# A two-layer network on one Trainium2 core: a new hand order for layer 1's scan, the image added to the rows during dispatch, and the last normalization batch in three stages

## Chip, cores and metric

The kernel runs on one core of one Trainium2 chip. A core has five engines that run their own instruction queues in order: PE (matrix products), DVE (vectors), ACT (activations and copies), POOL (vectors, and DMAs with computed addresses) and SP (DMA issue). They synchronise by semaphores. The metric is device time in microseconds (us), the median of repeated executions. One further execution was profiled; durations come from it.

## The reference, cut to what matters

The input is x, 32 images of 128 channels and 56 x 56 pixels, in float32. T = 32 x 3136 = 100352 tokens.

```python
# layer 0: convolution, normalization, mixture of experts
x = depthwise_conv7x7(input) + dw_bias                 # then channels last
x = (x - mean) / sqrt(var + 1e-6) * ln_gamma + ln_beta # per token, over channels
topv, topi = top_k(x @ Wg + bg, 2)                     # 8 experts, 2 per token
wts = softmax(topv)                                    # wts[:, 0] also ranks the tokens
# each expert takes its first int(1.25 * T / 8) tokens in rank order
y[e] = gelu(rows[e] @ W1[e] + b1[e]) @ W2[e] + b2[e]   # 128 -> 512 -> 128
out = input + x + layer_scale * sum_over_kept(gate * y)

# layer 1: two branches on x = out of layer 0
xh = cv1_w @ x + cv1_b
l = silu(batchnorm(depthwise_conv3x3(xh)))
t = layernorm(xh tokens)                               # 3136 tokens per image
xm, z = split(t @ in_proj_w.T)                         # 256 channels each
xm = silu(causal_conv4(xm) + conv1d_b)
dt, B, C = split(xm @ x_proj_w.T);  dt = softplus(dt @ dt_proj_w.T + dt_proj_b)
for each token: h = exp(dt * A) * h + dt * B * xm;  y = (h * C).sum(16 states)
g = ((y + xm * D) * silu(z)) @ out_proj_w.T
return x + cv2_w @ concat(l, g) + cv2_b
```

## The kernel before, in words

The kernel runs five stages one after the other.

*Convolution (start to about 1535 us).* The images are turned to pixels-by-channels in eight batches of four (`fill`), convolved on PE, and each batch is normalized while the next is convolved. `norm` handles 28 / 4 = 7 columns of 112 tokens at a time (a column is two image rows): DVE takes statistics (`bn_stats`, `bn_aggr`), ACT the square root, DVE its reciprocal `rs` and the shift `nm`, ACT writes the seven normalized columns into `xa`, POOL multiplies by `lng` and adds `lnb`, SP stores `xa` to the tensor `res_d` in memory, PE transposes `xa` and multiplies by the gate's weights, and DVE adds the bias to the logits. The tokens of a column come out of the convolution with each image row reversed. The last batch has no convolution beside it: its 16 norms run alone. The order of instructions outside layer 1 is made by the language's scheduler from the order of the program.

*Routing (to about 1775 us).* Top-2, gates and slots of all tokens on DVE and ACT, while SP fills the experts' buffer `buf_d` with zeros.

*Dispatch (1775 to 3940 us).* 56 steps (`QB` = 7 values of q, eight `p0` of 14 columns). SP loads a block of rows from `res_d` into `xg0`, ACT copies it to `xg1`, DVE writes each row's gate and its place for the way back (`bi`, made by an iota on POOL), and POOL issues 28 indirect DMAs (L859) that write 128 rows each to their slots in `buf_d`. There are six pairs of `xg` buffers. The weights of layer 1 are prepared in the middle (`weights`).

*Experts (3940 to about 5880 us).* For each 512 rows of `buf_d`: transposes, two products with a GELU between them, bias and gate, and POOL's indirect DMAs (L911) add the results to the tokens' rows in `res_d`.

*Layer 1 (about 5880 us to the end).* 224 groups g of 448 tokens (7 per image). For each group there are 16 units, one for each state i of the scan. A unit is: ACT's `exp_act` (two halves of 128 channels) into one of two PSUM buffers `da`, by turns; POOL's `db_pool`, one instruction for two units, `db` = `du` x B; DVE's `scan_dve`, the recurrence along the tokens; `cmul`, the product of the states with C (`cb`); `carry_act`, which copies the last state to the next group's start; and `sum_pe`, which adds the product to the group's sum in PSUM. `MODE` gives each unit a letter: D scans in place and multiplies on DVE; P scans into an SBUF buffer `hs` and multiplies on POOL; Q is P with the scan in two halves; M scans in two halves, with the product of the first half on DVE and of the second on POOL.

All other work of a group (`PLAN`: loading, the 1x1 convolution, normalization, projections, softplus, output) and of a unit (`UNITS`) has a place: a number in units of a sixteenth of a period, relative to the group's or the unit's start. The steps of all groups are sorted by place and issued in that order under a manual schedule, so the places set the order of every engine's queue, and nothing else: an engine does its next instruction as soon as what it needs is there.

```python
todo.append((DS * g + key, len(todo), names[name], (g, *args)))            # PLAN
todo.append((DS * g + i + key, len(todo), names[name], (DS * g + i, *args)))  # UNITS
todo.sort()
```

`fetch` loads the image block `x1` and the rows `yg` (from `res_d`); `moe_pe` adds them in PSUM, undoing the reversed rows with the permutation `perm`; `moe_act` copies the sum to `x1`. `du_pool` needs `dt`, which `sp_act` writes. `rstd_dve` (L1090, L1092, L1095), `te_dve` and `yz_dve` are the other DVE work.

Of the kernel before, what the change touches and what calls it, by code (L numbers as in the profile page):

```python
# [5 lines left out]
F32 = mybir.dt.float32  # L6
I32 = mybir.dt.int32
AF = mybir.ActivationFunctionType
# [34 lines left out]
MODE = 'DQDDQDPPDDDDPDDP'  # L43
PRODS = 6
PLAN = (
    (-41.157, "fetch"),
    (-34.382, "moe_pe"),
    (-32.986, "moe_act"),
    (-28.346, "cv1_pe", "p_cvc", "cv1c"),
    (-27.384, "sq_act"),  # L50
    (-26.393, "cv1_pe", "p_cv1", "cv1t"),
    (-25.274, "cv1_act"),
    (-23.306, "var_pe"),
    (-23.291, "rstd_act"),
    (-23.185, "edges_act"),
    (-20.935, "rstd_dve", 0),
    (-20.876, "rstd_dve", 1),
    (-19.458, "rstd_dve", 2),
    (-19.126, "bc_pe"),
    (-18.367, "te_dve"),  # L60
    (-18.165, "te_act"),
    (-17.77, "z_pe", 0),
    (-16.927, "z_copy", 0),
    (-15.982, "z_pe", 1),
    (-15.86, "xm_pe", 0),
    (-15.811, "xm_pe", 1),
    (-14.784, "z_copy", 1),
    (-14.441, "z_silu"),
    (-14.388, "xm_act", 0),
    (-14.349, "xm_act", 1),  # L70
    (-13.504, "tables"),
    (-13.487, "px_pe"),
    (-11.507, "px_act"),
    (-11.215, "dt_pe", 0),
    (-10.684, "dt_pe", 1),
    (-10.326, "sp_abs", 0),
    (-9.043, "sp_abs", 1),
    (-8.458, "sp_exp"),
    (-7.656, "sp_one"),
    (-6.228, "sp_w"),  # L80
    (-5.252, "sp_pe", ("w", "e", "m")),
    (-5.135, "sp_ln"),
    (-5.019, "sp_pe", ("u",)),
    (-4.678, "lt_pe", range(0, 9)),
    (-4.117, "sp_act", 0),
    (-3.918, "sp_act", 1),
    (-3.032, "lt_act", 0),
    (-3.001, "du_pool"),
    (-2.343, "lt_act", 1),
    (2.033, "lt_silu"),  # L90
    (3.656, "dd_pe"),
    (18.599, "yz_dve", 0),
    (18.857, "yz_dve", 1),
    (23.328, "out_pe"),
    (25.003, "out_act"),
# [3 lines left out]
        (-5.892, "bc_load", "bb"),  # L99
        (-3.501, "bc_load", "cb"),  # L100
        (-2.818, "db_pool"),
        (-0.991, "exp_act"),
        (-0.076, "scan_dve"),
        (0.16, "cmul", 0),
        (1.245, "carry_act"),
        (3.662, "sum_pe"),
    ),
    (
        (-2.505, "db_pool"),
        (-0.83, "exp_act"),  # L110
        (-0.619, "scan_dve"),
        (1.229, "cmul", 0),
        (3.088, "carry_act"),
        (9.441, "sum_pe"),
    ),
    (
        (-11.504, "bc_load", "bb"),
        (-2.533, "bc_load", "cb"),
        (-2.288, "db_pool"),
        (-0.633, "exp_act"),  # L120
        (-0.074, "scan_dve"),
        (0.16, "cmul", 0),
        (1.407, "carry_act"),
        (3.828, "sum_pe"),
    ),
    (
        (-3.007, "db_pool"),
        (-1.559, "exp_act"),
        (-0.609, "scan_dve"),
        (-0.338, "carry_act"),  # L130
        (0.16, "cmul", 0),
        (2.009, "sum_pe"),
    ),
    (
        (-4.093, "bc_load", "bb"),
        (-3.639, "db_pool"),
        (-0.666, "bc_load", "cb"),
        (-0.482, "exp_act"),
        (0.865, "scan_dve"),
        (1.06, "cmul", 0),  # L140
        (1.786, "sum_pe"),
        (2.033, "carry_act"),
    ),
    (
        (-4.025, "db_pool"),
        (-1.052, "exp_act"),
        (-0.068, "scan_dve"),
        (0.16, "cmul", 0),
        (1.263, "carry_act"),
        (3.791, "sum_pe"),  # L150
    ),
    (
        (-5.791, "bc_load", "bb"),
        (-4.743, "db_pool"),
        (-2.416, "bc_load", "cb"),
        (-0.463, "exp_act"),
        (0.538, "scan_dve"),
        (0.678, "cmul", 0),
        (1.758, "carry_act"),
        (4.239, "sum_pe"),  # L160
    ),
    (
        (-5.64, "db_pool"),
        (-0.299, "exp_act"),
        (-0.211, "scan_dve"),
        (1.06, "cmul", 0),
        (5.047, "sum_pe"),
        (5.187, "carry_act"),
    ),
    (  # L170
        (-7.178, "bc_load", "bb"),
        (-4.153, "db_pool"),
        (-3.514, "bc_load", "cb"),
        (-1.218, "exp_act"),
        (-0.956, "scan_dve"),
        (0.16, "cmul", 0),
        (0.466, "carry_act"),
        (0.815, "sum_pe"),
    ),
    (  # L180
        (-4.714, "db_pool"),
        (-1.825, "exp_act"),
        (-0.406, "scan_dve"),
        (0.16, "cmul", 0),
        (0.742, "carry_act"),
        (1.653, "sum_pe"),
    ),
    (
        (-8.23, "bc_load", "bb"),
        (-5.573, "bc_load", "cb"),  # L190
        (-4.053, "db_pool"),
        (-1.1, "exp_act"),
        (-0.6, "scan_dve"),
        (0.16, "cmul", 0),
        (0.996, "carry_act"),
        (1.077, "sum_pe"),
    ),
    (
        (-3.777, "db_pool"),
        (-0.685, "exp_act"),  # L200
        (-0.409, "scan_dve"),
        (0.16, "cmul", 0),
        (1.104, "sum_pe"),
        (1.278, "carry_act"),
    ),
    (
        (-7.87, "bc_load", "bb"),
        (-4.884, "bc_load", "cb"),
        (-4.31, "db_pool"),
        (-0.985, "exp_act"),  # L210
        (-0.749, "scan_dve"),
        (1.06, "cmul", 0),
        (5.159, "sum_pe"),
        (5.275, "carry_act"),
    ),
    (
        (-4.947, "db_pool"),
        (-0.443, "exp_act"),
        (0.085, "scan_dve"),
        (0.16, "cmul", 0),  # L220
        (0.197, "sum_pe"),
        (0.205, "carry_act"),
    ),
    (
        (-19.062, "bc_load", "bb"),
        (-4.926, "db_pool"),
        (-2.209, "bc_load", "cb"),
        (-1.206, "exp_act"),
        (-0.658, "scan_dve"),
        (0.16, "cmul", 0),  # L230
        (0.202, "sum_pe"),
        (0.903, "carry_act"),
    ),
    (
        (-3.892, "db_pool"),
        (-0.158, "exp_act"),
        (0.91, "scan_dve"),
        (1.06, "cmul", 0),
        (2.205, "carry_act"),
        (2.818, "sum_pe"),  # L240
# [4 lines left out]
def tile_kernel(tc: tile.TileContext, a: dict, out: bass.AP):  # L245
# [14 lines left out]
    with (  # L260
# [6 lines left out]
        res_d = dram.tile([T, C], F32, name="res_d")  # L267

        ident = const.tile([128, 128], F32, name="ident")
        make_identity(nc, ident)  # L270
        mean_w = const.tile([128, 128], F32, name="mean_w")
        nc.vector.memset(mean_w, 1.0 / C)

        perm = const.tile([TT, TT], F32, name="perm")
        nc.vector.memset(perm, 0.0)
        for k in (HW - 1, 3 * HW - 1):
            nc.gpsimd.affine_select(
                out=perm, in_=perm, compare_op=ALU.not_equal, fill=1.0, base=-k, pattern=[[1, TT]],
                channel_multiplier=1,
            )  # L280
# [23 lines left out]
        with (  # L304
# [48 lines left out]
            def conv(b, c0):  # L353
# [21 lines left out]
                for c in range(4):  # L375
# [9 lines left out]
                    dwb[:, c0 : c0 + 4].unsqueeze(2).unsqueeze(3).to_broadcast([TT, 4, NB0, NP]), ALU.add,  # L385
                )

            def norm(b, i, q):

                w = NP // 4  # L390
                o = i * (NP + 1) + q * w
# [63 lines left out]
            for b in range(NB + 1):  # L455
                work = []
                for i in range(NB0):
                    if b > 0:
                        work += [(norm, b - 1, i, q) for q in range(4)]
                    if b + 1 < NB:  # L460
                        work.append((fill, b + 1, i))
# [1004 lines left out]
```

## Time and profile before

| | |
|---|---|
| median of 12 runs | 15852.14 us (15846.65 to 15859.02) |
| the profiled execution | 15854.85 us, its span 15853.1 us |
| busy of the span | PE 81%, DVE 70%, ACT 66%, POOL 84% |
| mean granted TensorE clock | 0.913 |
| data moved by DMA | 2520.85 MB, 159 GB/s |
| costliest group | `db`<-`du`,`bb` on POOL, 1792 instructions, 6578.1 us, 3682 ns each |
| scan in place on DVE (L1373) | 2240 instructions, 4522.6 us, 2019 ns each |
| exp on ACT (L1354) | 7168 instructions, 4540.1 us, 637 ns each |
| product with C on DVE / POOL (L1397) | 2240, 1089 ns each / 1344, 1937 ns each |
| scatters of dispatch (L859) | 1568 instructions, 1645.6 us |
| scatter-adds of the experts (L911) | 984 instructions, 1584.1 us |

The busy shares are averages over stages with different limits; each stage has to be read by itself. A row of the timeline gives an instruction's start, its duration, engine, line, operation, output <- inputs with partitions x elements, and in square brackets the engine's idle time before it with what ended that. "PE" rows of 448 columns come in pairs, since a float32 product is two instructions.

### The profile page before, as it was taken

The numbers are of one execution on the slowest core, as the hardware profiler recorded it, in microseconds if no ns is written. First come the engines' busy times: TensorE is split into PE (matmuls) and PEld (weight loads), VectorE is DVE, ScalarE is ACT, GpSimd is POOL, SyncE is SP. The second block draws the span as 40 slices with busy tenths as digits, with TensorE's granted clock in tenths as the row PEclk, the third lists the DMA queues.
The fourth block names the chain that finished last, engine by engine and source line by source line (L and its number), as shares of the span: only waits on it lengthen the run. The fifth ranks groups of instructions, "written<-read, shape, count | busy, mean of one in ns | idle before, by whom it ended". The sixth has DMA issues, their size and how long they took to land. (4 is left out here: it accounts for less than half of the span.)

```text
span 15853.1 us, 247520 instructions
## 1 busy us (share of the span) xinstructions
PE 12823.8 (81%) x92981; PEld 7167.9 (45%) x92981; DVE 11117.4 (70%) x11366; ACT 10495.1 (66%) x21038; POOL 13323.4 (84%) x6330
## 2 busy tenths in 40 slices
PE   7996200000999999999999999999999999999998
PEld 7996100000777764444444444444444444444444
DVE  2655400000111119999999999999999999999999
ACT  4554300000444448888888888888888888888888
POOL 2443477777788879999999999999999999999999
PEclk9997555555999999999999999999999999999999
DMA  8785422222555545555555556555555555555555
GB/s 267 228 237 174 172 71 71 71 71 64 68 72 70 71 64 183 185 185 185 185 184 184 184 185 185 183 184 185 182 184 185 184 185 184 185 183 184 184 183 171
DMA packets 1325280, 2520.85 MB, mean 159 GB/s; under 512 B 139352, under 2 KB 777136, under 8 KB 1316400
## 3 DMA queue, kind: packets, MB, share of 16 engines
q1 hardware_dynamic: 1127600, 2310.57, 46.9%
q0 software_dynamic: 196480, 194.45, 7.2%
q8 instruction: 732, 11.99, 0.3%
q14 instruction: 468, 3.83, 0.1%
HBM read 2129.06 MB, written 375.43 MB: 158 GB/s over the span
## 5 line engine op out<-in xcount | busy, mean ns | idle before, releaser
L1336 POOL TENSOR_TENSOR db<-du,bb 128x1792 f32<-128x1792 f32 x1792 | 6578.1, 3682 | 0.6 <-DMA bb<-bc_d 0.5
L1354 ACT ACTIVATE da<-dt,aneg 128x449 f32<-128x449 f32 x7168 | 4540.1, 637 | 376.2 <-DVE r L1095 113.0
L1373 DVE TENSOR_TENSOR_SCAN da<-da,db 128x898 f32<-128x898 f32 x2240 | 4522.6, 2019 | 0.6 <-issue 0.5
L1286 PE MATMUL py<-prod,ident 64*64 64x448 f32 x28672 | 3223.9, 547 | 126.7 <-DVE prod L1397 118.7
L1397 POOL TENSOR_TENSOR prod<-hs,cb 128x896 f32<-128x896 f32 x1344 | 2603.5, 1937 | 243.5 <-issue 154.3
L1397 DVE TENSOR_TENSOR prod<-da,cb 128x896 f32<-128x896 f32 x2240 | 2439.8, 1089 | 136.3 <-DMA cb<-bc_d 20.7
L859 POOL DMA_INDIRECT buf_d<-xg,slot x1568 | 1645.6, 1049 | 523.8 <-issue 519.3
L911 POOL DMA_INDIRECT res_d<-ys,xb x984 | 1584.1, 1610 | 359.2 <-issue 278.9
L951 PE MATMUL ept<-ident,xb 128*128 128x128 f32 (+1 forms) x984 | 189.0, 274 | 2078.6 <-DMA xb<-buf_d 2078.3
L1373 DVE TENSOR_TENSOR_SCAN hs<-da,db 128x898 f32<-128x898 f32 x896 | 1785.5, 2013 | 0.1
L1286 PEld LDWEIGHTS py<-prod,ident 64*64 64x64 f32 x28672 | 1007.5, 132 | 1564.5 <-issue 1054.2
L1126 PE MATMUL p_xm<-te,wk 128*128 128x448 f32 x3584 | 1395.6, 540 | 0.0
L903 DVE TENSOR_TENSOR ys<-py,b2t 128x512 f32<-128x512 f32 (+2 forms) x256 | 170.9, 670 | 1735.9 <-PE py L897 1498.3
L856 DVE COPY xg<-gate 128x14 f32<-128x14 f32 x112 | 20.5, 186 | 1884.5 <-DMA buf_d<-xg,slot 1848.3
L854 ACT COPY xg<-xg 128x1792 f32<-128x1792 f32 x56 | 94.5, 1688 | 1821.7 <-DMA buf_d<-xg,slot 1772.8
L951 PEld LDWEIGHTS ept<-ident,xb 128*128 128x128 f32 (+1 forms) x984 | 124.6, 143 | 2082.4 <-issue 2081.6
L897 PEld LDWEIGHTS py<-w2t,hh 128*128 128x128 f32 x7872 | 939.1, 192 | 191.6 <-issue 118.4
L897 PE MATMUL py<-w2t,hh 128*128 128x128 f32 x7872 | 988.7, 279 | 14.9 <-ACT hh L893 9.5
L1126 PEld LDWEIGHTS p_xm<-te,wk 128*128 128x128 f32 x3584 | 671.8, 189 | 665.8 <-issue 568.0
L379 PE MATMUL pc<-xc,toep 112*112 112x112 f32 (+1 forms) x8192 | 937.4, 270 | 37.4 <-ACT toep L368 33.8
L1377 DVE TENSOR_TENSOR_SCAN hs<-da,db 128x449 f32<-128x449 f32 x896 | 925.5, 1075 | 0.5 <-ACT da L1354 0.3
L1258 PE MATMUL p_l<-xh,dwd 64*64 64x224 f32 x16128 | 907.0, 352 | 22.1 <-ACT dt L1240 2.2
(241 smaller groups left out, 20282.0 us busy)
## 6 DMA issues: line engine op xcount, KB each, us to landing
bb<-bc_d SPq DMA_DIRECT2D x1792, 448.0 KB
cb<-bc_d SPq DMA_DIRECT2D x1792, 448.0 KB
toep<-toep_d SPq DMA_DIRECT2D x448, 392.0 KB
buf_d<-zero SPq DMA_DIRECT2D x28, 2275.0 KB
xb<-buf_d SPq DMA_DIRECT2D x240, 260.0 KB
xt<-in_x SPq DMA_DIRECT2D x32, 1568.0 KB
res_d<-xa SPq DMA_DIRECT2D x128, 392.0 KB
xg<-res_d SPq DMA_DIRECT2D x56, 896.0 KB
```

The source lines that it names most:

```text
L379: nc.tensor.matmul(pc[:, c, :, lo:hi], lhsT=tp[c // 2][:, c % 2, 6 - 2 * o : 8 - 2 * o, :], rhs=s4[:, c, :, lo + o - 1 : hi + o - 1], star ...
L859: apart(nc.gpsimd.indirect_dma_start(out=buf_d[:, :], out_offset=bass.IndirectOffsetOnAxis(ap=slots[k][:, o + j : o + j + 1], axis=0), in_ ...
L897: nc.tensor.matmul(py[:n, j, :], lhsT=hh[:, k, j * 128 : j * 128 + n], rhs=w2t[:, k, :], start=k == 0, stop=k == KF - 1,)
L911: apart(nc.gpsimd.indirect_dma_start(out=res_d[:, :], out_offset=bass.IndirectOffsetOnAxis(ap=xb[:n, j, C + 1 : C + 2].bitcast(I32), axis= ...
L1126: nc.tensor.matmul(p[:, :CH1], lhsT=s["wk"][:, k, hs], rhs=d["te"][:, k : k + CH1], start=k == 0, stop=k == DC - 1 and not first,)
L1258: nc.tensor.matmul(d["p_l"][r][k * HD : (k + 1) * HD, : CH1 // 2], lhsT=s["dwd"][rs, t, rs], rhs=d["xh"][rs, dy + k * R : dy + (k + 1) * R ...
L1286: nc.tensor.matmul(ps[r][h * HD : (h + 1) * HD, :CH1], lhsT=lhsT(rs, h), rhs=rhs[rs, h, :], start=start, stop=stop,)
L1336: nc.gpsimd.tensor_tensor(dbp[i // 2].rearrange("p k (h t) -> p k h t", h=2)[:, :, :, 1:], st[g]["du"].unsqueeze(1).to_broadcast(both), un ...
L1354: e = nc.scalar.activation(da[:, h * W1 : (h + 1) * W1], st[g]["dt"][:, h, :], AF.Exp, scale=s["aneg"][:, h, i : i + 1])
L1373: scans.append(nc.vector.tensor_tensor_scan(hs, da, dbs[i], 0.0, ALU.mult, ALU.add))
L1377: scans.append(nc.vector.tensor_tensor_scan(hs2[h][:, hh], da[:, hh], dbs[i][:, hh], 0.0, ALU.mult, ALU.add))
L1397: eng.tensor_tensor(w["prod"], w["hs"][0][:, :, 1:], w["cb"], ALU.mult)
```

## The change

1. Layer 1's `MODE`, `PLAN` and `UNITS` get new values. `exp_act` and `scan_dve` take a half as an argument, so that each half has its own place; `hs` has three buffers instead of two, `x1` four instead of five. The dependencies that are declared absent between halves and between carries, scans and `db` are kept in one table (`free`, `decay`). The unit that closes the group's sum is the one whose `sum_pe` comes last.
2. In dispatch, after each step's scatters, `skip` is called once or twice: half an image (14 columns) and its rows are loaded, PE undoes the reversal of the rows with `perm` and adds the transposed image, ACT copies the result and issues its store to a new tensor `sum_d`. The experts add to `sum_d`, with places (`bi`) that count each row of 56 backwards. The copy of `xg0` to `xg1` goes from ACT to DVE. Layer 1's `fetch` loads from `sum_d` alone, and `moe_pe` is four transposes.
3. `norm` becomes a generator with two pauses. For the last batch, the 16 norms are advanced in a pipeline of three stages: statistics, normalized columns, logits. There, two of the seven columns are written by DVE instead of ACT.

```diff
-MODE = 'DQDDQDPPDDDDPDDP'
+MODE = 'PPDDMDPPDDPDPDDD'
 PLAN = (
-    (-41.157, "fetch"),
-    (-34.382, "moe_pe"),
+    (-60.5589, "fetch"),
+    (-32.6293, "moe_pe"),
...
-    (-4.117, "sp_act", 0),
-    (-3.001, "du_pool"),
+    (-3.7463, "sp_act", 0),
+    (-1.8387, "du_pool"),
...
 UNITS = (
     (
-        (-5.892, "bc_load", "bb"),
-        (-3.501, "bc_load", "cb"),
-        (-2.818, "db_pool"),
-        (-0.991, "exp_act"),
-        (-0.076, "scan_dve"),
-        (0.16, "cmul", 0),
-        (1.245, "carry_act"),
-        (3.662, "sum_pe"),
+        (-3.5445, "bc_load", "bb"),
+        (-0.1591, "exp_act", 1),
+        (0.0298, "db_pool"),
+        (0.2221, "exp_act", 0),
+        (1.0278, "scan_dve", 0),
+        (3.4411, "bc_load", "cb"),
+        (3.8013, "cmul", 0),
+        (4.9139, "sum_pe"),
+        (5.2017, "carry_act"),
     ),
...
             def norm(b, i, q):
+                for part in normal(b, i, q):
+                    pass
+
+            def normal(b, i, q):
...
                 nc.vector.scalar_tensor_tensor(nm, mv[:, :, 0], -1.0, rs, ALU.mult, ALU.mult)
+                yield
...
                 for j in range(w):
+                    if b == NB - 1 and j in (2, 5):
+                        nc.vector.tensor_scalar(
+                            xa[:, j, :], xv[:, :, j], rs[:, j : j + 1], nm[:, j : j + 1], ALU.mult, ALU.add
+                        )
+                        continue
                     nc.scalar.activation(
...
                     out=res_d[col * TT : (col + w) * TT, :].rearrange("(k p) c -> p k c", p=TT), in_=xa
                 )
+                yield
...
+                if b == NB:
+                    line = [normal(*w[1:]) for w in work]
+                    for k in range(len(line) + 2):
+                        for part in reversed(line[max(k - 2, 0) : k + 1]):
+                            next(part, None)
+                    work = []
...
-                nc.gpsimd.iota(bi, pattern=[[TT, QB], [1, TT]], base=0, channel_multiplier=PT)
+                nc.gpsimd.iota(
+                    bi.rearrange("p q (r w) -> p q r w", w=HW), pattern=[[TT, QB], [HW, 2], [-1, HW]], base=HW - 1,
+                    channel_multiplier=PT,
+                )
...
+            def skip(n, h):
+                t0 = (n * TPI + h * HT) * TT
+                xt = sk.tile([C, HT * TT], F32, name="xs")
+                nc.sync.dma_start(out=xt, in_=x_d[n, :, h * HT * TT : (h + 1) * HT * TT])
+                xr = sk.tile([TT, HT, C], F32, name="xr")
+                rows = [v[t0 : t0 + HT * TT, :].rearrange("(k p) c -> p k c", p=TT) for v in (res_d, sum_d)]
+                nc.sync.dma_start(out=xr, in_=rows[0])
+                for j0 in range(0, HT, 4):
+                    w = min(4, HT - j0)
+                    p = psk.tile([TT, 4, C], F32, name="p_sk")
+                    nc.tensor.matmul(p[:, :w], lhsT=perm, rhs=xr[:, j0 : j0 + w], start=True, stop=False)
+                    for j in range(w):
+                        nc.tensor.matmul(
+                            p[:, j, :], lhsT=xt[:, (j0 + j) * TT : (j0 + j + 1) * TT], rhs=ident,
+                            start=False, stop=j == w - 1,
+                        )
+                    nc.scalar.copy(xr[:, j0 : j0 + w], p[:, :w])
+                nc.scalar.dma_start(out=rows[1], in_=xr)
...
-                    nc.scalar.copy(xgs[1][:, :, :C], xgs[0][:, :, :C])
+                    nc.vector.tensor_copy(xgs[1][:, :, :C], xgs[0][:, :, :C])
...
+                    for _ in range(-(-len(parts) // (TT // XT * (QB - q) - p0 // XT))):
+                        skip(*parts.pop(0))
...
-                        out=res_d[:, :],
+                        out=sum_d[:, :],
...
-            d["x1"] = three.tile([C, CH1], F32, name="x1", bufs=5)
-            nc.sync.dma_start(out=d["x1"], in_=x_d[n, :, q * CH1 : (q + 1) * CH1])
...
-                out=d["yg"], in_=res_d[t0 : t0 + CH1, :].rearrange("(j p) c -> p j c", p=TT)
+                out=d["yg"], in_=sum_d[t0 : t0 + CH1, :].rearrange("(j p) c -> p j c", p=TT)
...
-            nc.tensor.matmul(p[:, :CH1], lhsT=ident, rhs=d["x1"], start=True, stop=False)
             for j in range(TPC1):
-                nc.tensor.matmul(
-                    p[:, j * TT : (j + 1) * TT], lhsT=yg[:, j, :], rhs=perm, start=False, stop=j == TPC1 - 1
-                )
+                nc.tensor.transpose(p[:, j * TT : (j + 1) * TT], yg[:, j, :], ident[:TT, :TT])
...
-            hs = three.tile([128, 2 * W1], F32, name="hs", bufs=2) if MODE[i] in "PQM" else da
+                hs = three.tile([128, 2 * W1], F32, name="hs", bufs=3)
```

Not shown: all other places, the bookkeeping of `free` and `decay`, `te_tile` (which lets `te_act` be issued before `te_dve`), and `mean_w`, which shrinks to one column.

## The prediction

> **What bounds the kernel now.** I read the busy slices first, then windows cut at the stages, then the timeline of each engine, engine by engine, inside one period of layer 1, inside the last normalization and inside dispatch. The slices show which engine fills each stretch (one digit is 396 us):
>
> ```profile
> DVE  2655400000111119999999999999999999999999
> POOL 2443477777788879999999999999999999999999
> ```
>
> Cut at the stages, the windows view (busy us and instructions of each engine, granted clock, DMA share, GB/s) reads:
>
> ```profile
> core 0: us, PE busy (x) PEld busy (x) DVE busy (x) ACT busy (x) POOL busy (x), PEclk, DMA share, GB/s
> 1400.00:1535.00 135.00, 69.63 (x336) 62.60 (x336) 65.11 (x267) 78.50 (x160) 67.08 (x33) 0.50 0.19 48
> 1775.00:3940.00 2165.00, 6.10 (x16) 2.87 (x16) 38.02 (x247) 95.55 (x63) 1644.54 (x1567) 0.50 0.24 72
> 3940.00:5880.00 1940.00, 1904.99 (x10842) 1375.58 (x10842) 347.65 (x529) 820.51 (x1241) 1581.88 (x983) 0.99 0.54 70
> 8000.00:12000.00 4000.00, 3829.76 (x28279) 1797.47 (x28274) 3941.05 (x3078) 3474.07 (x7204) 3839.77 (x1383) 1.00 0.58 184
> ```
>
> In the last batch's normalization no engine is over 60% busy: a chain of latencies. Dispatch is POOL alone, PE and ACT nearly empty. The experts are PE (98%) and the change leaves their instructions alone. Layer 1 takes 9970 of the 15853 us, with DVE at 98.5%, POOL and PE at 96%, ACT at 87%. A gain there must shorten DVE and leave POOL, 4% below it, room.
>
> One period of layer 1, DVE's timeline (start, duration, ...):
>
> ```profile
> 9009.88 2.03 DVE L1373 TENSOR_TENSOR_SCAN da<-da,db 128x898 f32<-128x898 f32 x1
> 9012.01 1.09 DVE L1397 TENSOR_TENSOR prod<-da,cb 128x896 f32<-128x896 f32 x1
> 9018.08 0.14 DVE L1090 SCALAR_TENSOR_TENSOR da<-da,r 112x4 f32<-112x4 f32 x1
> ...
> 9047.06 3.94 DVE L1373 TENSOR_TENSOR_SCAN hs<-da,db 128x898 f32<-128x898 f32 x2
> 9050.91 2.01 DVE L1373 TENSOR_TENSOR_SCAN da<-da,db 128x898 f32<-128x898 f32 x1
> ...
> 9062.22 0.14 DVE L1090 SCALAR_TENSOR_TENSOR da<-da,r 112x4 f32<-112x4 f32 x1
> ```
>
> L1090 runs once per group, so the period is 9062.22 - 9018.08 = 44.14 us, and DVE has no marked idle in it: DVE is the bound. Starts overlap ends, so I count from start to start. A scan followed by independent work costs 1.93 (3.85 for two, 9047.06 to 9050.91); followed by its own product it costs 2.04 to 2.13; a product 1.0; two half scans 1.98; two yz 1.17; te 0.52. POOL in the same period:
>
> ```profile
> 9003.58 3.68 POOL L1336 TENSOR_TENSOR db<-du,bb 128x1792 f32<-128x1792 f32 x1
> 9007.21 1.94 POOL L1397 TENSOR_TENSOR prod<-hs,cb 128x896 f32<-128x896 f32 x1
> 9062.87 1.94 POOL L1245 TENSOR_TENSOR du<-dt,xm 128x896 f32<-128x896 f32 x1 [0.81 <-ACT dt L1240]
> ```
>
> Start to start: db 3.64, product 1.89, du 1.92. Eight, six and one make 42.4 us, so POOL idles about 1.7 per period, partly for ACT's dt.
>
> **Part 1, layer 1's places and modes.** Six P, one M and nine D replace four P, two Q and ten D. *DVE:* nine and a half products for ten: -0.49. One pair of half scans for two: -0.05. Scans followed at once by their own product fall from seven to three (new order u5, u8, u15; the rest have a scan, yz, te or rstd between): 4 x 0.15 = -0.60. Together 44.14 - 1.14 = 43.0. *POOL:* adds M's half product. From the rows, (3682 - 1937)/896 = 1.95 ns an element and 0.19 fixed, so 448 elements take 1.07, 1.02 start to start: 42.4 + 1.0 = 43.4. POOL thus becomes the longest queue. *PE:* the product of x with the identity goes (two instructions, 1.0 us a group), and four transposes replace four matmuls with `perm`: in the trace a matmul is two instructions, the transposes at L349 one, so 1.05 us becomes 0.5. PE falls from 42.3 to 40.7. *SP:* one load of 224 KB less per group. *ACT:* one more tiny copy (M's carry), 38.4 as before.
>
> The floor is therefore 43.4. What can lift it are the crossings between queues; I walked the new order with start-to-start costs. POOL's order is db 0, 4, 2, 10, 6, products 0, 1, 4, db 8, products 6, 7, db 12, 14, product 10, du, product 12. The loop db 2, scans u2 to u12 on DVE (29.7), product 12 (1.9), next db 0, 4, 2 (10.9) makes 42.5 and three handovers: under the floor by 0.6. The queues that share ACT: du waits for the copies of dt, which stand behind the exps of u12, and those wait for scan u10. By the walk dt is ready 0.35 us before POOL gets to du. On ACT the stretch between scan u1's end and scan u7 holds the exps of u3 to u7, both table loads, silu, abs and small copies: 14.8 us start to start, against 14.6 of DVE. That is even, with slack elsewhere. I take 43.6, 0.2 above the floor: (44.14 - 43.6) x 224 = **-121**. Ends: the floor itself, -166; ACT late, see the rivals.
>
> The three `hs` buffers for two and five to four `x1` cost no time: POOL's product 0 ends before scan u6 asks for its buffer (by 4 us of the walk), and x1 is written only at `moe_act`. `fetch` stands 19 places earlier on SP; its buffer is free by then (`moe_pe` of two groups before, 4 places earlier), so nothing queues behind a wait.
>
> **Part 2, the last batch's normalization.** Timeline of the end of that stage:
>
> ```profile
> 1518.32 2.05 DVE L403 SCALAR_TENSOR_TENSOR nm<-mv,rs 112x7 f32<-112x7 f32 x1
> 1520.45 2.81 ACT L406 ACTIVATE xa<-xc,nm,rs 112x128 f32<-112x128 f32 x5 [4.22 <-POOL xa L410]
> 1525.19 2.07 POOL L409 TENSOR_TENSOR xa<-xa,lng 112x896 f32<-112x896 f32 x1 [4.84 <-ACT xa L406]
> ```
>
> The DVE instruction for nm, 0.15 us elsewhere, takes 2.05 while POOL's product runs, and ends with it; ACT waits for it, POOL for ACT. POOL's two products and that wait make 9.0 us per norm; from the first sqrt (1400.66) to the last logits (1534.2) 16 norms take 133.5. In the pipeline nm is made a step earlier, so a step is the longest engine: POOL 4.15; ACT five xa (0.56 each), sqrt and copies, 4.0; DVE statistics 2.9, nm, logits and two tensor_scalars (0.21 each, as at L750), 3.9. POOL waits for the two tensor_scalars, so 4.9; with two steps of fill 18 x 4.9 = 88: **-45**. Ends: POOL alone, 18 x 4.3, -56; nm and both tensor_scalars each held for most of a POOL product, 18 x 7, -7. Everything after this stage (top-2, routing, zero fill) moves with it.
>
> **Part 3, the image added in dispatch.** 64 skips, two in each of the first 8 steps and one in the other 48. On PE one is 3.5 x 0.89 (a 512-wide matmul, from L890) + 14 x 0.25 (L897) = 6.6 us, 13 at the granted clock of 0.50 that this stage shows: under 850 us in 2165 where PE does nothing. ACT gives up a copy of 1.69 per step and gets four copies of about 0.6 per skip and the issue of the store. DVE takes the copy: about 1.3 us (tensor_scalar on 784 elements is 0.56), behind which the gate and place copies queue, six steps ahead of their use. SP queues two loads of 0.8 MB behind each xg load; an xg load of 0.9 MB fills the DMA engines for 3 to 4 us, so a buffer's round is load 7, PE 13, store 5, or 13 us per skip with two buffers, so two skips (26) fit in a step of 28 scatters (35.5). The last step's skip is loaded six steps ahead like its xg, so its store is done before the experts add to `sum_d`. `perm` moves in front of the first scatter: two POOL instructions of 0.3.
>
> Does 154 MB more traffic slow the scatters? The windows of POOL's scatters alone (busy, instructions, clock, DMA share, GB/s):
>
> ```profile
> 1775.00:2035.00 260.00, 197.80 (x205) 0.50 0.33 95
> 2100.00:3660.00 1560.00, 1181.50 (x1114) 0.50 0.24 71
> 3725.00:3935.00 210.00, 162.85 (x152) 0.50 0.15 48
> ```
>
> The pace is 1.27 us, then 1.40, and 1.38 in the last window, where the xg loads are over: less traffic, same pace, and the fastest stretch had most traffic. I take no cost for the traffic and **+5** for the late first scatter and `perm`. Ends: 0, and 56 x 1.3 = +73 if POOL stood still for every DVE copy. The row against that:
>
> ```profile
> 1828.40 1.46 DVE L750 TENSOR_SCALAR dwd<-ident,dw 128x128 f32<-128x128 f32 x7
> 1828.40 0.97 POOL L859 DMA_INDIRECT buf_d<-xg,slot  x1 [0.30 <-issue]
> ```
>
> Seven copies-with-scale on DVE, and the scatter takes its usual 0.97. The Trainium skill, "DMA: Bandwidth & Descriptors", section "SWDGE vs HWDGE vs iDMA", speaks against the move: VectorE in a two-port mode locks GpSimd out of the memory in which it writes descriptors. By it the sum would end nearer to the +73; by the row it stays at +5.
>
> **Sum.** The profiled execution took 15854.85 us (span 15853.1 and 1.75 around it), 2.7 above the median. 15854.85 - 121 - 45 + 5 = 15693.9; I say 15694 and leave the 2.7 in the range.
>
> **Rivals.** *The gain of layer 1 is eaten by handovers:* POOL at 99.5% leaves no room, each late dt or cb load (33.6 and 20.7 us of waits for cb in the whole run) now counts, and the period stays between 43.8 and 44.15. Then 15740 to 15815. For it: two queues within 1% of each other. Against: before, DVE ran a whole period without a gap.
>
> *ACT becomes the bound, and the kernel is slower:* place, ACT between the exps of u3 and u7. If its instructions cost their listed durations and not the start-to-start distances, the stretch is 16.0 and the period 44.4; each us over 14.6 costs 224. It decides from 15.9 (period about 44.3, which eats the -40 of the other parts); at 16.5 the time is 15855 + 179 - 40 = 15994. Against: before, ACT ran 33 us on end in the same way and held DVE up nowhere.
>
> *Transfers hold the scatters up:* 192 more of them, 3.5 us each; if POOL stood still in all, +672, about 16370. It decides from 0.84 us per transfer. Against: the pace without loads.
>
> *The pipeline isn't one:* the order outside layer 1 is made at build time, and the old order may come back: 15739, inside the range.
>
> **How the numbers follow.** Forecast (period 43.4 to 43.8, norm gain 7 to 56, dispatch 0 to 73) 0.67; handovers 0.19; ACT 0.10; transfers 0.04. 0.2% (32 us) is about what a measurement can tell from none: faster means under 15820. From the forecast and nearly all of the handover case 0.85; same 0.04; slower 0.11. The range reaches from floor and best pipeline (15635) to the end of the handover case (15815).
>
> **What would show it.** In the changed profile: L1090 every 43.6 us; POOL over 98.5% and DVE near 98.5% in layer 1, ACT's exps waiting for DVE and not DVE's scans for ACT; p_moe transposes of one instruction; POOL's two products every 4.9 us in the last norms; scatters at 1.40 with 140 GB/s around them. I am wrong if DVE's scans show waits for ACT's da or POOL's db of over 0.5 us a period, or if dispatch is longer than 2240.

## The result: 0.93% slower

The kernel after takes 15999.59 us (median of 7 runs, 15985.08 to 16016.95) against 15852.33 us for before (28 runs): a ratio of 1.0093, 95% interval 1.0084 to 1.0102. The forecast was 15694 us, faster. The profiled execution of after has a span of 15993.7 us, 140.6 more than before.

Cut by the first and last scatter and the first and last scatter-add, the two traces differ so (us; the predicted change beside it):

| stretch | before | after | change | predicted |
|---|---|---|---|---|
| start to the first scatter | 1773.6 | 1742.3 | -31 | -45 |
| first to last scatter (dispatch) | 2164.5 | 2372.1 | **+208** | +5 |
| last scatter to last scatter-add (experts) | 1943.0 | 1942.2 | -1 | 0 |
| last scatter-add to the end (layer 1) | 9971.9 | 9937.1 | -35 | -121 |

All three estimates were too good, but dispatch alone turned the sign. The slices of after (one digit is 400 us):

```profile
DVE  2657300000111117999999999999999999999999
POOL 2443455657788888999999999999999999999999
```

From the sixth to the ninth digit (2000 to 3600 us) POOL has fallen from 7 to 5 or 6: this is dispatch, which consists of POOL's work, and POOL now stands still in it. The windows view of after, with the columns of before's (busy us, instructions, clock, DMA share, GB/s):

```profile
1742.00:4115.00 2373.00, 584.29 (x2320) 396.47 (x2320) 90.51 (x319) 137.22 (x264) 1538.25 (x1568) 0.59 0.45 131
8000.00:12000.00 4000.00, 3799.21 (x27758) 1741.06 (x27761) 3903.28 (x2994) 3469.89 (x7310) 3937.21 (x1478) 1.00 0.57 179
```

POOL's own work in dispatch became shorter (1538 us for 1645) while the stage became longer. In layer 1 POOL went from 96.0% to 98.4% and VectorE from 98.5% to 97.6%: the busiest engine moved, the period hardly did.

**Where dispatch waits.** The waits view of after between 1760 and 4114 us (engine, line, what it waited for: us in total, times, longest):

```profile
POOL buf_d L916 <- DMA xg<-res_d: 352.8, 16, 43.0
```

```profile
ACT xr L900 <- remote: 1154.2, 83, 29.0
```

POOL waits for its rows, ACT for something that the profile calls remote. One such wait, on the timelines of SP, PE, ACT and POOL in turn (start, duration, ...; the bracket is the idle time before it):

```profile
2626.81 0.32 SPq L890 DMA_DIRECT2D xr<-res_d  x1
2677.86 0.33 SPq L887 DMA_DIRECT2D xs<-in_x  x1
2678.49 0.37 SPq L910 DMA_DIRECT2D xg<-res_d  x1
```

```profile
2624.42 1.02 PE L894 MATMUL p_sk<-xr,perm 112*112 112x512 f32 x2
2625.29 1.04 PE L896 MATMUL p_sk<-ident,xs 128*112 128x128 f32 x8
```

```profile
2630.93 0.59 ACT L900 COPY xr<-p_sk 112x512 f32<-112x512 f32 x1 [13.70 <-remote]
2651.22 0.59 ACT L900 COPY xr<-p_sk 112x512 f32<-112x512 f32 x1 [19.70 <-remote]
2675.72 0.59 ACT L900 COPY xr<-p_sk 112x512 f32<-112x512 f32 x1 [23.91 <-remote]
```

```profile
2689.28 1.27 POOL L916 DMA_INDIRECT buf_d<-xg,slot  x1 [18.58 <-DMA xg<-res_d]
```

In these rows L887 loads the image block (`xs`), L890 the skip's rows (`xr`) and L910 the rows to scatter (`xg`); the copies at L900 each wait for one chunk of TensorE's work (`p_sk`). Read it backwards. POOL lacks its xg at 2670.7 because SP issued that load only at 2678.49; SP stood for 51 us in front of it at a load of x, whose buffer TensorE had not finished reading. TensorE's rows say that the third chunk (2624.42 to 2626.3) was done at 2626.3; the copy that waits for nothing but that chunk starts at 2675.72. The ends of matmuls are modelled in these rows, and here they are wrong by 49 us: the trace has the semaphore that TensorE raises behind this chunk at 2675.70, so TensorE was not done. Where several skips queue, the copies follow one another every 28.0 us for a chunk of 10 matmul instructions (1861.56, 1889.56, 1917.57) and every 16.8 us for one of 6. That is 2.8 us for one matmul instruction, so a skip of 36 takes 101 us, not the 13 of the prediction. When POOL stops, TensorE catches up: in 16 of the 17 stops the waiting copies follow one another every 0.5 to 3 us from 6 to 8 us after the last scatter on (in the first, from 24 us on). Of the 256 copies, 191 fall into the 361 us of stops or the 20 us after each.

This is not new in after. In before TensorE does a little work during dispatch, the weights of layer 1; ACT and PE:

```profile
1869.34 0.37 ACT L821 COPY wo<-p_wo 128x256 f32<-128x256 f32 x1 [4.96 <-remote]
```

```profile
1864.01 1.23 PE L817 MATMUL p_wo<-cvgt,wop 128*128 128x128 f32 x4
```

Four instructions of 1.23 us in all, and the copy came 5.3 us after their start, 1.3 us an instruction, 90 us after the first scatter. The prediction took its price of a matmul from the experts' rows and halved the clock; the row of the right stage lay a few lines away. It shows half of the price paid later, but well over the 0.28 us that the experts' 128 x 128 products show (L897).

### The profile page after: what moved, and what is told of

It is laid out like the page before. It is cut to its first block, busy times and chain, and to the rows that moved or that the text cites. A ratio compares the mean times of both kernels' runs of the same rounds, so it can differ in the third digit from the quotient of the medians.

```text
span 15993.7 us, 248874 instructions
## 1 busy us (share of the span) xinstructions
PE 13307.1 (83%) x93941; PEld 7418.9 (46%) x93941; DVE 11067.9 (69%) x11231; ACT 10477.4 (66%) x21398; POOL 13431.3 (84%) x6554
## 5 line engine op out<-in xcount | busy, mean ns | idle before, releaser
L1433 DVE TENSOR_TENSOR_SCAN da<-da,db 128x898 f32<-128x898 f32 (+1 forms) x2240 | 4273.4, 1926 | 54.3 <-ACT da L1417 52.0
L1433 DVE TENSOR_TENSOR_SCAN hs<-da,db 128x898 f32<-128x898 f32 (+1 forms) x1568 | 2914.3, 1882 | 112.5 <-ACT da L1417 88.7
L916 POOL DMA_INDIRECT buf_d<-xg,slot x1568 | 1538.8, 981 | 837.0 <-issue 468.4
L1446 DVE TENSOR_TENSOR prod<-da,cb 128x896 f32<-128x896 f32 x2016 | 2185.8, 1084 | 43.7 <-DMA cb<-bc_d 6.0
L970 POOL DMA_INDIRECT sum_d<-ys,xb x984 | 1590.2, 1616 | 352.3 <-issue 279.2
L894 PE MATMUL p_sk<-xr,perm 112*112 112x512 f32 (+1 forms) x512 | 342.2, 759 | 1266.5 <-issue 758.7
L900 ACT COPY xr<-p_sk 112x512 f32<-112x512 f32 (+1 forms) x256 | 134.6, 533 | 1749.3 <-remote 1155.7
L1012 ACT COPY xc<-ept 128x512 f32<-128x512 f32 (+1 forms) x248 | 144.1, 581 | 1382.5 <-PE ept L1010 664.3
L383 PEld LDWEIGHTS pc<-xc,toep 112*112 112x112 f32 x8192 | 884.5, 185 | 45.4 <-ACT toep L372 39.1
L949 PE MATMUL ph<-xc,w1t 128*128 128x512 f32 (+1 forms) x1984 | 886.5, 589 | 0.0
```

What stands on the lines that cost most here:

```text
L383: nc.tensor.matmul(pc[:, c, :, lo:hi], lhsT=tp[c // 2][:, c % 2, 6 - 2 * o : 8 - 2 * o, :], rhs=s4[:, c, :, lo + o - 1 : hi + o - 1], star ...
L894: nc.tensor.matmul(p[:, :w], lhsT=perm, rhs=xr[:, j0 : j0 + w], start=True, stop=False)
L916: apart(nc.gpsimd.indirect_dma_start(out=buf_d[:, :], out_offset=bass.IndirectOffsetOnAxis(ap=slots[k][:, o + j : o + j + 1], axis=0), in_ ...
L949: nc.tensor.matmul(ph[:, :rows], lhsT=w1t[:, k * 128 : (k + 1) * 128], rhs=xc[:, :rows], start=True, stop=True)
L970: apart(nc.gpsimd.indirect_dma_start(out=sum_d[:, :], out_offset=bass.IndirectOffsetOnAxis(ap=xb[:n, j, C + 1 : C + 2].bitcast(I32), axis= ...
L1433: scan = nc.vector.tensor_tensor_scan(w["hs"][h][:, hh], da[:, hh], dbs[i][:, hh], 0.0, ALU.mult, ALU.add)
```

## The experiments

Theory: beside the scatters TensorE passes one matmul instruction per 2.8 us, skips don't fit in their steps, their loads hold SP's queue, and xg comes late. Rivals: the 154 MB more traffic; the longer SP queue by itself; VectorE's copy of xg.

**1. Fewer TensorE instructions, same transfers.**

```diff
-                    nc.tensor.matmul(p[:, :w], lhsT=perm, rhs=xr[...], start=True, stop=False)
-                    for j in range(w):
-                        nc.tensor.matmul(p[:, j, :], lhsT=xt[...], rhs=ident, start=False, stop=j == w - 1)
+                    nc.tensor.matmul(p[:, :w], lhsT=perm, rhs=xr[...], start=True, stop=True)
```

> The kernel after with the 14 products of x with the identity left out of every skip, so the image isn't added; every DMA of the skip (two loads, one store), ACT's copies and the product with perm stay. TensorE has 8 matmul instructions per skip left of 36 to 38. Theory 1, TensorE is slow while scatters run: in the trace of after, copies that wait for TensorE follow one another every 28.0 us for a chunk of 10 matmul instructions and every 16.8 us for one of 6, that is 2.8 us an instruction, and at once when POOL stands still. Then a skip takes 22 us instead of about 105, fits in a step of 28 scatters, POOL's waits for xg fall from 353 us to under 60, the scatters last 1990 to 2170 us instead of 2372 and the kernel takes 15620 to 15800 us. Theory 2, the traffic or SP's queue: nothing of either is taken away, so POOL waits for xg as before, scatters 2370 us, the kernel 15990 to 16005 us.

Measured: 15781.54 us, 218 less than after; scatters 2166.7 us long; no wait of POOL for xg is left, and the copies come every 5.6 us in the mean for 2 instructions, again 2.8 each:

```profile
2574.42 0.59 ACT L895 COPY xr<-p_sk 112x512 f32<-112x512 f32 x1 [5.93 <-remote]
2579.32 0.58 ACT L895 COPY xr<-p_sk 112x512 f32<-112x512 f32 x1 [4.32 <-remote]
2585.62 0.58 ACT L895 COPY xr<-p_sk 112x512 f32<-112x512 f32 x1 [5.71 <-remote]
```

Traffic and SP's queue, all of it still there at 143 GB/s, and VectorE's copy cost the scatters nothing. All three rivals fall.

**2. TensorE work beside scatters, without the skips.**

```diff
+            def extra(k):
+                p = psk.tile([128, 4 * C], F32, name="p_sk")
+                cols = [C, 4 * C, C][k // 19]
+                for j in range(5 if k < 38 else 10):
+                    if k < 38:
+                        nc.tensor.matmul(p[:, :cols], lhsT=ident, rhs=wide[:, :cols], start=j == 0, stop=j == 4)
+                    else:
+                        nc.tensor.transpose(p[:, j % 4 * C : (j % 4 + 1) * C], wide[:, :C], ident)
+                sc = sk.tile([128, 4 * C], F32, name="sc")
+                nc.scalar.copy(sc[:, :cols], p[:, :cols])
```

> The kernel before with the copy of xg on VectorE, and in each of the 56 steps of dispatch one chunk of TensorE work on constants that nothing else waits for, copied out by ACT: steps 0 to 18 five f32 products 128 wide (10 matmul instructions), 19 to 37 five 512 wide (10, four times the columns), 38 to 55 ten transposes 128 wide (10). No skip, no traffic of it. Theory 1 (an instruction of TensorE takes 2.8 us beside scatters, whatever its width): the copies follow one another every 28 us in all three forms. Theory 1b (per column): 28 us or less in the first and third, over 80 in the second. Theory 2 (only the traffic of the skips made it slow): all three complete in the time of their records, 3 to 9 us a chunk. The time of the kernel is that of the run with the copy alone.

Its timelines of ACT and PE in the second form, and PE in the third:

```profile
2055.91 0.59 ACT L860 COPY sc<-p_sk 128x512 f32<-128x512 f32 x1 [26.02 <-remote]
2084.61 0.59 ACT L860 COPY sc<-p_sk 128x512 f32<-128x512 f32 x1 [28.11 <-remote]
```

```profile
2056.55 7.32 PE L856 MATMUL p_sk<-wide,ident 128*128 128x512 f32 x10 [19.64 <-ACT sc L860]
2408.80 2.40 PE L858 MATMUL p_sk<-ident,wide 128*128 128x128 f32 x10 [27.00 <-issue]
```

26.6 to 29.4 us from copy to copy in all three forms, so four times the columns, or transposes, make no difference; the number of instructions does. The first eight copies, right after the first scatter, came 1.1 to 2.1 us apart, and it took until 1860 us, 90 us of scatters, to reach 28. The traffic here was 76 GB/s from 1850 to 2170 us, as in the same stretch of before. The time, 15873.84 us in one run, is 23 above that of the copy alone (next). The weights of layer 1 also wait for TensorE, behind the added chunks: VectorE stood 199 us for one of their products, its copies of xg behind that, and POOL stopped for 42 us at 2177. In that stop and for 20 us behind it TensorE was fast again, 4.3 us a chunk of 512-wide products.

**3. VectorE's copy alone.**

```diff
-                    nc.scalar.copy(xgs[1][:, :, :C], xgs[0][:, :, :C])
+                    nc.vector.tensor_copy(xgs[1][:, :, :C], xgs[0][:, :, :C])
```

> The kernel before with one edit: the copy of xg for the second gate in dispatch on VectorE instead of ACT. In before the scatters go at 1.27 us and from 230 us on at 1.40, two slow ones in every 16 or 17; in after they go at 1.27 wherever POOL doesn't wait. Theory A, ACT's copy makes the slow ones: they vanish, dispatch 1568 x 1.27 = 1991 us instead of 2165, the kernel 15680 us. Theory B, a backlog: POOL issues a scatter every 1.27 us, they complete every 1.40, and the waits of after gave the backlog time to drain: the pace stays at 1.40, the kernel within 20 us of 15852. If VectorE's copies stopped POOL by their length, 56 x 1.1 = 60 us slower.

Measured: 15851.09 us, ratio 1.0003 [0.9993, 1.0012]; scatters 2167.4 us long. VectorE's copy costs the kernel nothing that can be measured and gains nothing, so theory A falls. It does hold the scatter beside it; VectorE and POOL in this run:

```profile
1960.17 1.09 DVE L854 COPY xg<-xg 128x1792 f32<-128x1792 f32 x1 [17.59 <-DMA buf_d<-xg,slot]
```

```profile
1958.80 0.97 POOL L859 DMA_INDIRECT buf_d<-xg,slot  x1 [0.31 <-issue]
1960.07 1.32 POOL L859 DMA_INDIRECT buf_d<-xg,slot  x1 [0.30 <-issue]
1961.69 0.97 POOL L859 DMA_INDIRECT buf_d<-xg,slot  x1 [0.30 <-issue]
```

The scatter ends 0.12 us after the copy. Nearly all scatters that meet one of the 56 copies end 0.12 or 0.83 us after it and take 1.33 us in the median, some 27 us in all; the stage is no longer for it.

In after the long scatters (up to 1.9 us for 0.97) are nearly gone all the same, 29 of over 1.4 us for 128 in before, and 27 of the 29 stand beside VectorE's copies. That is why 361 us of stops cost only 208: before loses 179 us to long ones (2164.5 less 1567 steps of 1.267). In every run without stops, dispatch took 2165 to 2168 us, at 72 GB/s or at 143. That speaks for a backlog, theory B, but not all of it fits: after its last stop, which ends at 3612 us, after runs 500 us at 1.28, while before had its first long ones 287 us after the first scatter. What makes them stays open.

**4. The other two parts on the old dispatch**, first together, twice, then the normalization alone.

```diff
-    (-60.5589, "fetch"),
+    (-41.157, "fetch"),
...
-            d["yg"] = two.tile([TT, TPC1, C], F32, name="yg")
+            d["x1"] = three.tile([C, CH1], F32, name="x1", bufs=5)
+            nc.sync.dma_start(out=d["x1"], in_=x_d[n, :, q * CH1 : (q + 1) * CH1])
+            d["yg"] = two.tile([TT, TPC1, C], F32, name="yg", bufs=1)
```

> The kernel before with two parts of the change alone: the last batch's normalization in three stages and layer 1's new modes and places; dispatch and the fetch of x in layer 1 stay as before (fetch at its old place, one buffer for yg instead of two so that three hs fit). Theory: the parts add up as the trace of after shows them, -31 for the normalization and -35 for layer 1: 15786 us. Rival: layer 1's 35 us came from the load and the two TensorE instructions that the skip took out of each period: then 15821 us. The sum that was predicted for the two parts: 15852 - 121 - 45 = 15686 us.

Measured: 15879.85 us, ratio 1.0018 [1.0009, 1.0028], worse than each expectation. The normalization's gain is there (first scatter 1739.8); layer 1's period is 44.41 us. Its waits between 8000 and 12000 us:

```profile
DVE yz L1324 <- PE py L1334: 65.4, 90, 1.3
```

0.73 us per period, which after does not have (7.0 us there in all). With x back on TensorE, the new places make yz late. So after's layer 1 is a sum of two: the new places cost 224 x (44.41 - 44.14) = 60 us, and taking x out gains 224 x (44.41 - 43.99) = 94.

A second run with both parts (`norm_l1_early`) has TensorE's product for the fetched rows at its old, earlier place, and besides the three moves that section 5 tries on after. Expected were 15767 us or less if the later place had made yz late, and 15860 to 15880 if TensorE's whole work with x binds wherever the product stands. Measured: 16135.36 us, ratio 1.0178 [1.0162, 1.0193], period 45.54, beyond both. The wait of yz is gone (7.1 us in all), but `te`, another VectorE step, now waits for TensorE, a wait that none of the other runs shows:

```profile
DVE te L1158 <- PE p_bc L1145: 54.4, 88, 0.6
```

The three moves alone make 44.84 (section 5); with x on TensorE the period is 0.70 us longer, and this wait is 0.62 of it. The earlier product seems only to hand the wait on, which speaks for TensorE's work on x as the cost. The load of x, the place of `fetch` and the second buffer of `yg`, which differ too, were not tried apart.

> The kernel before with the last batch's normalization in three stages, and nothing else. In the trace of after the first scatter starts 31 us earlier than in before (1742.3 for 1773.6), and with it 33 us earlier where layer 1's part was added too (1739.8). Theory: that is the whole effect and it survives to the end: 15852 - 32 = 15820 us. As predicted for this part: -45, 15807 us. Rival: what comes after takes it back (the routing or the first loads): over 15840 us.

The diff is the change's own in `normal` and its loop. Measured: 15814.77 us, ratio 0.9977 [0.9968, 0.9986]: faster than both kernels, 37 us less than the runs of before beside it; the first scatter (1742.4) shows 31 of them.

**5. What holds layer 1's period.** Three moves together; mode D for unit 4; then one of the moves by itself.

```diff
-    (-22.6002, "rstd_act"),
-    (-22.4112, "rstd_dve", 0),
-    (-22.4112, "rstd_dve", 1),
+    (-23.2700, "rstd_act"),
+    (-22.9000, "rstd_dve", 0),
+    (-22.9000, "rstd_dve", 1),
...
-    (-19.7814, "edges_act"),
+    (-19.7300, "edges_act"),
```

> The kernel after with three places of layer 1 moved: ACT's square root of the variance in front of softplus's second step, the first two VectorE steps of it in front of the scan of unit 9, and the copies of the edges behind the copies of dt. In after's trace ACT's exp of unit 10 waits 0.69 us for VectorE's step, the copies of dt end 0.5 us after POOL is ready for du, and VectorE waits 0.26 and 0.39 us for exps. Theory, the period hangs on ACT's chain to dt: it falls from 43.99 us to between 43.4 (POOL's own work) and 43.7, the kernel by 65 to 130 us, to 15870 to 15935 us. Rival, another cycle binds as well (POOL's db, VectorE's scans): period 43.9 to 44.0, 15980 to 16000 us.

Measured: 16209.18 us, period 44.84. ACT's moved square root writes a small tile (`aside`, L1151) that lies in unit 8's buffer `da`; it now comes ahead of VectorE's product of unit 8, which waits for it 1.1 us a period:

```profile
DVE prod L1446 <- ACT da L1151: 99.8, 89, 1.3
```

One wait was exchanged for a longer one; the theory was not tested.

```diff
-MODE = 'PPDDMDPPDDPDPDDD'
+MODE = 'PPDDDDPPDDPDPDDD'
...
-        (0.705, "scan_dve", 1),
...
-        (1.0371, "cmul", 1),
```

> The kernel after with unit 4 in mode D instead of M: its whole product and one whole scan on VectorE, half a product less (1.0 us a period) on POOL, about 0.45 more on VectorE. If POOL's own 43.4 us sets layer 1's period of 43.99, it falls to 43.6 or less, 15915 us. If VectorE and its waits set it, it rises by about 0.45 to 44.4, 16090 us. If the chain over ACT to dt sets it, neither matters: 43.9 to 44.1, 15980 to 16020 us.

Measured: 16248.12 us in one run, period 45.14. POOL lost 1.0 us of work and the period rose by 1.15, so POOL's own work does not set it here. The rise is more than VectorE's 0.45: the scan of unit 4, now whole, waits for both halves of its exp, 0.85 us a period, where in after the first half scan waits 0.23 (20.6 us in all) for one half:

```profile
DVE da L1431 <- ACT da L1415: 76.1, 89, 1.0
```

```diff
-    (-19.7814, "edges_act"),
+    (-19.7300, "edges_act"),
```

> The kernel after with one place of layer 1 moved: ACT's copies of the edges (0.27 us) behind the copies of dt instead of in front of them; the two other moves of the earlier run are left out. In after POOL is ready for du 0.5 us before dt is copied. If that wait sets the period, it falls by up to 0.27 us, from 43.99 to 43.7, the kernel by 50 to 60 us to 15940 to 15950. If the loop of VectorE's scans and products with ACT's exps sets it (two da buffers, VectorE's waits of 0.26 and 0.39 us), dt 0.27 us earlier only makes POOL wait elsewhere: 43.95 to 44.05, within 15 us of after.

Measured: 15993.35 us (ratio to before 1.0095; after 1.0093), period 43.98. The waits of POOL for dt (in after the first line, put down to VectorE's product, which ends 0.07 us after dt; in this run the second):

```profile
POOL du L1318 <- DVE prod L1446: 42.1, 75, 1.1
```

```profile
POOL du L1318 <- ACT dt L1313: 24.2, 85, 0.8
```

POOL's wait fell by 0.2 us a period and nothing came of it: POOL stood in front of its next products instead (33.6 us for 5.4). With the run before, this leaves the loop of VectorE's scans and products with ACT's exps as what sets the period. That is a conclusion by elimination: no run shortened this loop alone.

**6. A skip with few instructions, complete.** Layer 0 already has the image turned in PSUM; its tiles are copied out and stored a second time.

```diff
+                    xw = cp.tile([TT, 4, C], F32, name="xw", bufs=2)
+                    nc.vector.tensor_copy(xw[:, :w], p[:, :w])
+                    nc.scalar.dma_start(out=xrow_d[r0 : r0 + w * TT, :].rearrange("(k p) c -> p k c", p=TT), in_=xw[:, :w])
...
-                    for j in range(w):
-                        nc.tensor.matmul(p[:, j, :], lhsT=xt[...], rhs=ident, start=False, stop=j == w - 1)
-                    nc.scalar.copy(xr[:, j0 : j0 + w], p[:, :w])
+                    nc.vector.tensor_tensor(xr[:, j0 : j0 + w], p[:, :w], xt[:, j0 : j0 + w], ALU.add)
```

> The kernel after with the image turned into rows where layer 0 has it turned already: VectorE copies each turned tile out of PSUM a second time, ACT's queue stores it (256 stores of 229 KB), and a skip loads these rows in place of x, has TensorE make only the product with perm (8 matmul instructions for 36 to 38) and VectorE add. The whole computation is there. By the pace of 2.8 us an instruction a skip takes 22 us of TensorE and fits: scatters 2165 to 2180 us long, and where layer 0 takes the copies and stores beside its work, the kernel takes 15780 to 15800 us, below the 15815 of the normalization alone. Layer 0's first batches have TensorE at 90% and more and wait for both copies: if each second copy (0.7 us) and each store (0.35 us of ACT) holds the turning up, 256 x 1 = 256 us more, 16040.

Measured: 16008.29 us. Scatters 2166.5 us long, with the whole image added: 8 instructions per skip fit, as theory 1 says. But the first scatter starts at 1960.6 for 1742.3: layer 0 pays 218 us for the second copies and stores. The bad end of the expectation was the right one in size. The wait in its way is another than it priced, the one for the store of the copy's buffer, of which there are two (start to 1400 us):

```profile
DVE xw L358 <- DMA xrow_d<-xw: 215.4, 103, 8.3
```

**7. The held pieces of the normalization.**

```diff
-                    if b == NB - 1 and j in (2, 5):
-                        nc.vector.tensor_scalar(xa[:, j, :], xv[:, :, j], rs[...], nm[...], ALU.mult, ALU.add)
-                        continue
```

> The kernel with the normalization in three stages alone, but with all seven pieces of a norm on ACT, as in the other batches, instead of five on ACT and two on VectorE. In after's last norms POOL's pairs of products start alternately 4.6 and 7.1 us apart, 5.7 in the mean where 4.9 was predicted, and pieces on VectorE take up to 3.5 us for 0.35 beside POOL's products. If these held pieces make the long steps, the steps even out at what ACT needs, 7 x 0.56 + 1.1 = 5.0 to 5.3 us, and the first scatter starts 6 to 10 us earlier than 1742.4. If VectorE's nm (2.0 us when held) or the statistics do, the steps stay at 5.7 or get longer, since ACT has more to do, and the first scatter starts at 1742 or later. The kernel's time moves by under 0.1% either way.

Measured: the steps fall from 5.67 to 5.17 us in the mean, 7.4 us in 15 steps, so the held pieces (the 3.5 us of the expectation are two of them) make part of the long steps; 4.7 and 5.7 still alternate. The first scatter starts at 1738.0, 4.4 us earlier than in the run with the pieces on VectorE; but in the eight runs with this normalization and the pieces on VectorE it lies anywhere from 1737.2 to 1745.9, so it can't show the gain. Nor can the time, 15812.91 us in one run.

## Why the prediction was wrong

**Dispatch, the step that failed.** "13 at the granted clock of 0.50", "so two skips (26) fit in a step of 28 scatters (35.5)". The clock was as assumed or better (0.59 over the stage); the pace was not set by it. A skip takes 101 us beside scatters. "No cost for the traffic" was right (run 1). So was no cost for VectorE's copy, a ratio of 1.0003 in run 3, but the row that it was taken from misled: there a tensor_scalar left the scatter at 0.97 us, while run 3's copies hold the scatter beside them to 1.33. That is what the Trainium skill, "DMA: Bandwidth & Descriptors", section "SWDGE vs HWDGE vs iDMA", warned of; the rows agree with it, and the kernel's time shows no cost. The rival for transfers had +208 within its reach (1.08 us for each of its 192 transfers), but by another mechanism: no transfer holds the scatters up, TensorE holds the transfers up. The prediction's own test, dispatch longer than 2240, was met, and so was the other: VectorE's scans wait 0.61 us a period for ACT's `da`.

**Layer 1, mis-sized: -121 was -35.** The handover rival had the size: a period of 43.8 to 44.15, measured 43.99 in the mean. POOL's 43.4 came out as summed (3937.21 busy in 4000, 43.3 a period). VectorE's 43.0 came out near 43.3, and then it waits for exps. Its timeline in after:

```profile
9031.05 1.10 DVE L1433 TENSOR_TENSOR_SCAN da<-da,db 128x449 f32<-128x449 f32 x1 [0.26 <-ACT da L1417]
...
9047.47 2.03 DVE L1433 TENSOR_TENSOR_SCAN hs<-da,db 128x898 f32<-128x898 f32 x1 [0.39 <-ACT da L1417]
```

```profile
9046.12 1.31 ACT L1417 ACTIVATE da<-dt,aneg 128x449 f32<-128x449 f32 x2 [0.69 <-DVE da L1160]
...
9051.65 0.96 ACT L1313 COPY dt<-p_sp 128x448 f32<-128x448 f32 x2
```

```profile
9052.69 1.93 POOL L1318 TENSOR_TENSOR du<-dt,xm 128x896 f32<-128x896 f32 x1 [0.51 <-DVE prod L1446]
```

The two half scans of unit 4 take 2.72 us with their product where 2.5 was summed; the scans of units 4 and 10 wait 0.65 in all, the second because ACT's exp waits for `rstd_dve`, which the walk had not followed across engines; du waits 0.5 where the walk had dt ready 0.35 early. The step that failed is the 0.2 us that the walk had for all crossings together; they are worth 0.6. The ACT rival named the right engine, and the exp of unit 4 lies in its stretch, but the longer wait, at unit 10, does not. And the PE line, "from 42.3 to 40.7", counted as room, was worth more than the part's whole gain: with x still on TensorE, the new places lose 60 us (run 4).

**Normalization, mis-sized: -45 was -31.** The stages overlap as said, POOL's pairs start 5.67 us apart in the mean for the 4.9 of the sum and 7.9 in before (the 9.0 that the prediction read are every second one there). The two VectorE pieces were priced at 0.21 each; POOL and VectorE in after:

```profile
1438.64 2.09 POOL L423 TENSOR_TENSOR xa<-xa,lng 112x896 f32<-112x896 f32 x1 [2.92 <-ACT xa L420]
```

```profile
1439.55 3.48 DVE L416 TENSOR_SCALAR xa<-xc,rs,nm 112x128 f32<-112x128 f32 x2
```

Both are held while POOL multiplies, 3.48 us for the 0.7 of undisturbed pairs, and in the first ten steps those of 4.6 us alternate with ones of 6 to 7. That was the bad end of the range (7 a step); the value lay between.

## What to carry to other kernels

Price an instruction from rows of the stage into which it is moved, and for TensorE by when its consumer starts: "TensorE idle in this stage" says nothing of its pace there. Before a load is put ahead of another on one queue, ask which slow reader frees its buffer, because that reader then stands in front of everything behind it. Where two engines are within 1% of each other, sum the crossings, not only the queues, and see whether the freed engine was the one with the waits.

## What the runs showed of the hardware

Beside indirect scatters of 128 rows of 520 bytes, TensorE completed one matmul instruction per 2.8 us (28.0 us for 10), at 128 and at 512 columns and for transposes alike, with 75 to 143 GB/s of traffic around them. Each of these has a weight load of its own (2320 of both in after's dispatch). It took 90 us of scatters to set in, and the pace is the same whether the scatters go at 1.40 us (run 2) or at 1.27 (after). In the experts, beside scatter-adds at one per 1.9 us, 10783 matmuls took 1906 us, so indirect transfers at that rate don't do it. Which resource the two share was not found out. The two queues that load the engines' programs show nothing of it: in run 2 their 27 packets between 1800 and 3900 us took at most 1.3 us each. TensorE's own rows hide it: ten matmuls are drawn as 2.40 or 7.32 us. The Trainium skill, "Perfetto Trace Analysis", in its opening note, calls matmul busy time a bad measure of how close a kernel is to the roofline, because matmuls are pipelined; here the drawn time is too short by 21 to 26 us of 28.
